# A graph network of four layers: the identity of the third layer added into its adjacency tiles, and a column of logits summed on VectorE

## The chip, the cores and the metric

The kernel runs on one core of one Trainium2 chip, as one program. Its metric is the device time in microseconds, of which the median of several runs is given. A core has TensorE (matrix products, into PSUM), VectorE, ScalarE and GpSimd (element-wise work), and queues that start transfers between the memory of the chip (HBM) and the memory of the core (SBUF). In the profile TensorE is PE, its weight loads are PEld, VectorE is DVE, ScalarE is ACT.

## What is computed

Four layers on 4096 nodes with 128 features each, over one 4096 × 4096 adjacency matrix; each layer's result is added to its input and normalised by rows. The first layer is a hyperbolic attention, the second an attention with four heads. The change is in the third, a convolution, and in what prepares the fourth, an attention with additive logits. From the reference:

```python
def _L2_gnn_ref(x, adj, weight):                  # the third layer
    n = adj.shape[0]
    adj_hat = adj + jnp.eye(n, dtype=adj.dtype)
    deg = jnp.sum(adj_hat, axis=1)
    d_inv_sqrt = (deg + 1e-08) ** (-0.5)
    support = d_inv_sqrt[:, None] * adj_hat * d_inv_sqrt[None, :]
    out = jnp.matmul(jnp.matmul(support, x), weight)
    return jax.nn.relu(out)

def _L3_gnn_ref(X, A, W, b, a_s, a_r):            # the fourth layer
    H = X @ W.T + b
    s = H @ a_s
    r = H @ a_r
    e = jax.nn.leaky_relu(A * s + A * r.T, negative_slope=ALPHA)
    masked = jnp.where(A > 0, e, NEG)
    att = jax.nn.softmax(masked, axis=1)
    return att @ H

# each layer: x = _layernorm(x + layer(x), axis=-1)
```

Two things matter. The third layer uses the adjacency plus the identity. And the fourth layer needs, for every node, the two scalars `s` and `r`; `r` is X times the vector `W.T @ a_r`, plus a constant.

## The kernel before

The adjacency lies in HBM as 8 × 8 tiles of 512 × 512, `adjT[I, J]`, each 1 MB: 128 partitions by four blocks of 512. A ring of eight tiles in SBUF is filled ahead. For each row of tiles I, `convolve` sums over J into one PSUM tile `pa` of 128 features by 512 nodes. `Y` holds the features, scaled by the inverse square root of the degree. The identity of `adj_hat` is added by four matmuls of `Y` with a 128 × 128 identity at the start of the row. `odd` looks, for half of the tiles, whether all entries are 0 or 1.

```python
def convolve(I, J):
    if J == 0:
        st["pa"] = open_sums()
        for b in range(4):
            nc.tensor.matmul(                                              # L1326
                st["pa"][:, b * P : (b + 1) * P], lhsT=Y[:, 4 * I + b, :], rhs=self.ident,
                start=(b == 0), stop=False, skip_group_check=True,
            )
    at = ring[:, (NS * I + J) % RING, :, :]
    for jb in range(4):
        nc.tensor.matmul(                                                  # L1332
            st["pa"], lhsT=Y[:, 4 * J + jb, :], rhs=at[:, jb, :],
            start=False, stop=(J == NS - 1 and jb == 3), skip_group_check=True,
        )
    if J < NS // 2:
        odd = rot.tile([P, 4, S], F32, tag="odd", name="odd", bufs=1)
        n = 2 * NT + NS // 2 * I + J
        nc.vector.scalar_tensor_tensor(                                    # L1340
            odd, at, 0.0, at, op0=ALU.not_equal, op1=ALU.not_equal, accum_out=self.odd[:, n : n + 1]
        )
```

A finished row is worked up in pieces, one piece after each of the tiles J = 0, 1, 2, 3, 5, 6 of the next row:

```python
def finish(I):
    ...
    nc.scalar.copy(a, st["pa"])                                            # L1369, after J = 7
    yield
    pb = ps_b.tile([P, 4, D], F32, tag="pb", name="pb")
    for b in range(4):                                                     # L1373, after J = 0
        nc.tensor.matmul(pb[:, b, :], lhsT=a[:, b * P : (b + 1) * P], rhs=w, start=True, stop=True)
    ...                                                                    # o = relu(d * pb), on ScalarE
    yield
    nc.vector.tensor_tensor(x, x, o, ALU.add)                              # L1378, after J = 1
    for b in range(4):
        self.row_stats(4 * I + b)
    nc.vector.tensor_scalar(rs, self.mv[:, tl, 1], EPS_LN, None, op0=ALU.add)   # L1381
    ...                                                                    # rs = rs ** -0.5, on ScalarE
    yield
    for b in range(4):                                                     # L1387, after J = 2
        ...                                                                # X = (X - mean) * rs
    yield
    for b in range(4):                                                     # L1393, after J = 3
        nc.tensor.transpose(p[:, b, :], X[:, 4 * I + b, :], self.ident)
    nc.scalar.activation(XT, p..., AF.Identity, accum_out=part[:, I : I + 1])
    nc.vector.tensor_tensor(XB[:, tl, :], x, br..., ALU.add)               # L1395
    yield
    pr = ps_s.tile([P, S], F32, tag="ps", name="pr")                       # after J = 5
    for b in range(4):
        nc.tensor.matmul(                                                  # L1399
            pr[:, b : b + 1], lhsT=XT[:, b * P : (b + 1) * P], rhs=ur, start=True, stop=True
        )
    ps = ps_s.tile([P, S], F32, tag="ps", name="psr")
    nc.tensor.matmul(ps, lhsT=us, rhs=XT, start=True, stop=True)           # L1403
    nc.vector.tensor_scalar(r, pr[:, 0:4], cb[:, 1:2], 2.0 * LIMIT, op0=ALU.add, op1=ALU.min)   # L1405
    ...
    nc.vector.tensor_scalar(rho[:, s], ps, cb[:, 0:1], 2.0 * LIMIT, op0=ALU.add, op1=ALU.min)   # L1408
    nc.vector.tensor_reduce(mx[...], rho[:, s], AX.X, ALU.max, apply_absolute_value=True)       # L1409
    ...
    yield
    ...                                                                    # F = X * exp(r), after J = 6
```

The loop runs over 64 tiles of the third layer and then the first eight tiles of the fourth (`attend_first`, L1352 and L1355), during which the last row of the third is finished:

```python
for g in range(groups):                       # groups = NS * NS + NS = 72
    I, J = g // NS, g % NS
    if I < NS:
        convolve(I, J)
    else:
        attend_first(J)
    load(g + RING - 1)
    if g == 2:
        weights()                             # us, ur, cb; L1292 to L1304
    ...
    if J in (0, 1, 2, 3, 5, 6):
        next(rest, None)
    if J == NS - 1 and I < NS:
        rest = finish(I)
        next(rest)
```

Of the kernel before, what the change touches and what calls it, by code (L numbers as in the profile page):

```python
# [9 lines left out]
F32 = mybir.dt.float32  # L10
F32R = mybir.dt.float32r
AF = mybir.ActivationFunctionType
ALU = mybir.AluOpType
# [3 lines left out]
P = 128  # L17
# [7 lines left out]
S = 512  # L25
SAFE = 60.0
LIMIT = 20.0
# [14 lines left out]
class Net:  # L42
# [1201 lines left out]
    def layers23(self, w2, weight, bias, a_s, a_r, out, Y):  # L1244
# [5 lines left out]
        nc, tc, N, NT, NS, D, X = self.nc, self.tc, self.N, self.NT, self.NS, self.D, self.X  # L1250
        with ExitStack() as ctx:
            RING = 8
# [12 lines left out]
            pre = pctx.enter_context(tc.tile_pool(name="pre3", bufs=1))  # L1265
# [11 lines left out]
                nc.sync.dma_start(out=ac[:, k : k + 1], in_=v.unsqueeze(1))  # L1277
            us = pre.tile([P, P], F32, tag="us", name="us")
            ur = pre.tile([P, 1], F32, tag="ur", name="ur")
            cb = pre.tile([P, 2], F32, tag="cb", name="cb")  # L1280
            wt = pre.tile([P, P], F32, tag="wtr", name="wtr")
            last = pre.tile([P, P], F32, tag="last", name="last")
# [4 lines left out]
            st = {}  # L1287

            def weights():

                p = ps_t.tile([P, 4, P], F32, tag="pt", name="pu")
                nc.tensor.matmul(p[:, 0, 0:2], lhsT=wn, rhs=ac[:, 0:2], start=True, stop=True)  # L1292
                nc.tensor.matmul(
                    p[:, 1, 0:2], lhsT=ac[:, 2:3].to_broadcast([P, P]), rhs=ac[:, 0:2], start=True, stop=True
                )
                nc.vector.tensor_copy(us, p[:, 0, 0:1].to_broadcast([P, P]))
                nc.vector.tensor_copy(ur, p[:, 0, 1:2])
                nc.vector.tensor_copy(cb, p[:, 1, 0:2])


                p = ps_t.tile([P, 4, P], F32, tag="pt", name="pw")
                nc.tensor.transpose(p[:, 0, :], wn, self.ident)
                nc.vector.tensor_copy(wt, p[:, 0, :])
                nc.vector.tensor_copy(last, self.ident[:, D - 1 : D].to_broadcast([P, P]))  # L1304
                st["pw"] = p
# [12 lines left out]
            def open_sums():  # L1318
                return ps_a.tile([P, S], F32, tag="pa", name="pa")

            def convolve(I, J):

                if J == 0:
                    st["pa"] = open_sums()
                    for b in range(4):
                        nc.tensor.matmul(  # L1326
                            st["pa"][:, b * P : (b + 1) * P], lhsT=Y[:, 4 * I + b, :], rhs=self.ident,
                            start=(b == 0), stop=False, skip_group_check=True,
                        )
                at = ring[:, (NS * I + J) % RING, :, :]  # L1330
                for jb in range(4):
                    nc.tensor.matmul(  # L1332
                        st["pa"], lhsT=Y[:, 4 * J + jb, :], rhs=at[:, jb, :],
                        start=False, stop=(J == NS - 1 and jb == 3), skip_group_check=True,
                    )
                if J < NS // 2:

                    odd = rot.tile([P, 4, S], F32, tag="odd", name="odd", bufs=1)
                    n = 2 * NT + NS // 2 * I + J
                    nc.vector.scalar_tensor_tensor(  # L1340
                        odd, at, 0.0, at, op0=ALU.not_equal, op1=ALU.not_equal, accum_out=self.odd[:, n : n + 1]
                    )

            def attend_first(J):

# [13 lines left out]
            def finish(I):  # L1359


                s, tl = slice(I * S, (I + 1) * S), slice(4 * I, 4 * I + 4)
                x = X[:, tl, :]
                a = rot.tile([P, S], F32, tag="a", name="a")
                o = rot.tile([P, 4, D], F32, tag="o", name="o")
                rs = rot.tile([P, 4], F32, tag="rs", name="rs")
                XT = rot.tile([P, S], F32, tag="XT", name="XT")
                r = rot.tile([P, 4], F32, tag="r", name="r")
                nc.scalar.copy(a, st["pa"])  # L1369
# [5 lines that stand above are left out]
                    t = 4 * I + b  # L1375
                    nc.scalar.activation(o[:, b, :], pb[:, b, :], AF.Relu, scale=d[:, t : t + 1])
                yield
                nc.vector.tensor_tensor(x, x, o, ALU.add)  # L1378
# [3 lines that stand above are left out]
                nc.scalar.activation(rs, rs, AF.Ln)  # L1382
                nc.scalar.activation(rs, rs, AF.Exp, scale=-0.5)
                yield
                for b in range(4):
                    t = 4 * I + b
                    nc.vector.tensor_scalar(  # L1387
                        X[:, t, :], X[:, t, :], self.mv[:, t, 0:1], rs[:, b : b + 1], op0=ALU.subtract, op1=ALU.mult
                    )
                yield  # L1390
                p = ps_t.tile([P, 4, P], F32, tag="pt", name="pt")
                for b in range(4):
                    nc.tensor.transpose(p[:, b, :], X[:, 4 * I + b, :], self.ident)  # L1393
                nc.scalar.activation(XT, p.rearrange("p a b -> p (a b)"), AF.Identity, accum_out=part[:, I : I + 1])
                nc.vector.tensor_tensor(XB[:, tl, :], x, br.unsqueeze(1).to_broadcast([P, 4, D]), ALU.add)  # L1395
                yield
                pr = ps_s.tile([P, S], F32, tag="ps", name="pr")
                for b in range(4):
                    nc.tensor.matmul(  # L1399
                        pr[:, b : b + 1], lhsT=XT[:, b * P : (b + 1) * P], rhs=ur, start=True, stop=True  # L1400
                    )
                ps = ps_s.tile([P, S], F32, tag="ps", name="psr")
                nc.tensor.matmul(ps, lhsT=us, rhs=XT, start=True, stop=True)  # L1403

                nc.vector.tensor_scalar(r, pr[:, 0:4], cb[:, 1:2], 2.0 * LIMIT, op0=ALU.add, op1=ALU.min)  # L1405
                nc.vector.tensor_scalar(r, r, -2.0 * LIMIT, None, op0=ALU.max)
                nc.vector.tensor_reduce(mx[:, I : I + 1], r, AX.X, ALU.max, apply_absolute_value=True)
                nc.vector.tensor_scalar(rho[:, s], ps, cb[:, 0:1], 2.0 * LIMIT, op0=ALU.add, op1=ALU.min)  # L1408
                nc.vector.tensor_reduce(  # L1409
                    mx[:, NS + I : NS + I + 1], rho[:, s], AX.X, ALU.max, apply_absolute_value=True  # L1410
                )
                nc.scalar.activation(col[:, 0, tl], r, AF.Exp, scale=-0.8)
                nc.scalar.activation(col[:, 1, tl], r, AF.Exp)
                nc.scalar.activation(rho[:, s], rho[:, s], AF.Exp, scale=0.8)
                yield
                for t in range(4 * I, 4 * I + 4):
                    nc.scalar.activation(F[:, t, 0 : D - 1], X[:, t, 0 : D - 1], AF.Copy, scale=col[:, 1, t : t + 1])
                nc.vector.tensor_copy(F[:, tl, D - 1], col[:, 1, tl])
# [19 lines left out]
            with tc.manual_schedule():  # L1438
                nc.scalar.preload_act_table_set("natural_log_exp_and_others")
                for g in range(RING - 1):  # L1440
                    load(g)
                for g in range(groups):
                    I, J = g // NS, g % NS
                    if I < NS:
                        convolve(I, J)
                    else:
# [3 lines that stand above are left out]
                        weights()  # L1450
                    if g == 4:
                        weights_last()
# [6 lines that stand above are left out]
                    if g == groups - 2:  # L1459
                        close_first()  # L1460
                nc.tensor.matmul(st["pa3"], lhsT=tot, rhs=eps, start=False, stop=True, skip_group_check=True)
                nc.scalar.copy(a0, st["pa3"])
# [166 lines left out]
```

## Time and profile before

| | |
|---|---|
| time, median of 3 runs | 2186.93 us (2184.12 to 2188.29) |
| span in the profile | 2182.5 us |
| TensorE busy | 2000.2 us, 92% |
| VectorE busy | 1849.3 us, 85% |
| ScalarE busy | 1458.3 us, 67% |
| third layer, from its first matmul to the first of the fourth layer | 1675.5 to 1926.8 us |
| tile matmuls (L1332) | 512 records, mean 594 ns, no idle time before them |
| identity matmuls (L1326) | 64 records, median 275 ns |
| column of logits (L1399) | 64 records, median 250 ns |

A record is one instruction as the profiler saw it; a matmul in fp32 of this kernel shows as two records, and records of neighbouring matmuls overlap, so the cost of a matmul is read from one start to the next and not from its duration. In the chain of work that ended last, each piece is what the piece after it had to wait for; a piece counts for the time only if it stands there.

### The profile page before, as it was taken

The page shows a single profiled execution, that of the slowest core. Times are in us where ns is not written, and L with a number is a line of the kernel's source. Part 1 is how long each engine was busy: PE and PEld are TensorE (multiplying, and loading weights), DVE is VectorE, ACT ScalarE, POOL GpSimd, SP SyncE. Part 2 cuts the span into 40 slices and gives each one's busy share as a digit, 9 for nine tenths or more (in the row PEclk, how much of TensorE's full clock was granted, in tenths as well). Part 3 has the DMA queues.
Part 4 walks back from the last instruction along what each step waited for, and adds up shares of the span by engine and source line. Part 5 has one row for each costly group of instructions (what it writes and reads, how often), then busy time and mean ns, then how long its engine had stood idle before and what let it go on. Part 6 is the DMA issues. An engine that isn't in the chain of part 4 may idle for free.

```text
span 2182.5 us, 24442 instructions
## 1 busy us (share of the span) xinstructions
PE 2000.2 (92%) x8876; PEld 1066.8 (49%) x8876; DVE 1849.3 (85%) x2700; ACT 1458.3 (67%) x1847; POOL 120.4 (6%) x204
## 2 busy tenths in 40 slices
PE   4699999999999717999999999999997999999998
PEld 4267767776766605333333333333333444544443
DVE  6699999999999887789899999999898454568887
ACT  5699999999999783787878787887883222210000
POOL 2100000000000022210000000000000000000000
PEclk8599999999999957999999999999999999999999
DMA  3166666666666407984645565564555877767783
GB/s 94 55 238 225 214 218 227 217 227 210 210 243 208 159 1 251 240 223 174 193 170 179 175 202 178 176 192 174 175 193 208 312 265 273 261 247 285 288 296 112
DMA packets 114455, 446.77 MB, mean 205 GB/s; under 512 B 12108, under 2 KB 22508, under 8 KB 73360
## 3 DMA queue, kind: packets, MB, share of 16 engines
q1 hardware_dynamic: 93120, 359.77, 46.6%
q10 hardware_dynamic: 9360, 68.16, 9.2%
q0 software_dynamic: 11840, 17.13, 4.4%
q8 instruction: 74, 1.21, 0.2%
q14 instruction: 61, 0.50, 0.1%
HBM read 367.34 MB, written 77.68 MB: 204 GB/s over the span
## 4 chain that ended last, share of the span: by engine, by line
PE 43%; DVE 31%; ACT 16%; DMA 5%; issue 4%; SPq 0%; POOL 0%; ACTq 0%; DVEq 0%; POOLq 0%
PE pa L1332 10%; PE pv L994 10%; PE pa L1512 9%; DVE e L977 8%; PE ps L968 6%; ACT e L975 4%; DVE w L686 3%; DMA adjT<-at 2%; ACT w L674 2%; DVE nat L958 2%; DVE w L718 2%; DVE t L705 2%; DVE w L729 2%; DVE t L666 2%; DVE at L645 2%
## 5 line engine op out<-in xcount | busy, mean ns | idle before, releaser
L977 DVE SCALAR_TENSOR_TENSOR e<-at,e 128x2048 f32<-128x2048 f32 x256 | 582.9, 2287 | 69.6 <-ACT e L975 68.9
L975 ACT ACTIVATE e<-ps 128x1024 f32<-128x1024 f32 x512 | 493.2, 1024 | 145.6 <-PE ps L968 126.0
L994 PE MATMUL pv<-e,VA 128*64 128x512 f32 x2048 | 495.8, 605 | 6.4 <-DVE e L977 6.0
L968 PE MATMUL ps<-QS,KS 128*128 128x512 f32 x1024 | 313.5, 425 | 5.2 <-ACT e L975 3.0
L968 PEld LDWEIGHTS ps<-QS,KS 128*128 128x128 f32 x1024 | 171.3, 189 | 230.2 <-ACT e L975 174.8
L994 PEld LDWEIGHTS pv<-e,VA 128*64 128x64 f32 x2048 | 124.6, 136 | 249.3 <-issue 214.9
L1332 PE MATMUL pa<-ring,Y 128*128 128x512 f32 x512 | 225.8, 594 | 0.0
L1512 PE MATMUL pa<-w,F 128*128 128x512 f32 x448 | 195.3, 594 | 0.0
L1509 DVE SCALAR_TENSOR_TENSOR w<-rho,col,ring 128x512 f32<-128x512 f32 x224 | 162.7, 745 | 22.9 <-PE pa L1512 10.3
L641 PE MATMUL ptA<-ident,ad 128*128 128x128 f32 x1024 | 154.0, 280 | 16.2 <-DMA ad<-in_adj_dram 9.4
L657 PE MATMUL pz<-HT 128*128 128x512 f32 x288 | 159.8, 638 | 1.5 <-DVE e L463 0.9
L741 PE MATMUL pi<-HA,w 128*128 128x129 f32 x1152 | 154.5, 282 | 2.8 <-DVE w L718 2.8
L1332 PEld LDWEIGHTS pa<-ring,Y 128*128 128x128 f32 x512 | 96.0, 191 | 111.5 <-issue 111.3
L741 PEld LDWEIGHTS pi<-HA,w 128*128 128x128 f32 x1152 | 138.2, 193 | 20.5 <-issue 17.2
L686 DVE TENSOR_TENSOR w<-w,at 128x2048 f32<-128x2048 f32 x64 | 146.3, 2285 | 0.0
L1512 PEld LDWEIGHTS pa<-w,F 128*128 128x128 f32 x448 | 83.7, 190 | 106.1 <-issue 77.6
L641 PEld LDWEIGHTS ptA<-ident,ad 128*128 128x128 f32 x1024 | 119.0, 143 | 29.5 <-issue 15.7
L949 ACT ACTIVATE nat<-nat 128x2048 f32<-128x2048 f32 x64 | 122.6, 1916 | 3.9 <-DMA nat<-in_adj_dram 3.8
L666 DVE TENSOR_SCALAR t<-pz 128x512 f32<-128x512 f32 x144 | 96.1, 686 | 16.5 <-PE pz L660 12.8
L756 PE MATMUL pj<-HA,w 128*128 128x129 f32 x896 | 109.7, 275 | 0.1
L756 PEld LDWEIGHTS pj<-HA,w 128*128 128x128 f32 x896 | 104.4, 191 | 0.7 <-DVE X L770 0.3
L645 DVE COPY at<-ptA 128x512 f32<-128x512 f32 x128 | 87.2, 686 | 11.9 <-PE ptA L641 7.1
(392 smaller groups left out, 2514.7 us busy)
## 6 DMA issues: line engine op xcount, KB each, us to landing
ring<-adjT SPq DMA_DIRECT2D x128, 1024.0 KB, 4.9
ad<-in_adj_dram SPq DMA_DIRECT2D x64, 1024.0 KB, 7.1
adjT<-at SPq DMA_DIRECT2D x64, 1024.0 KB, 6.1
nat<-in_adj_dram ACTq DMA_DIRECT2D x64, 1024.0 KB, 4.9
at<-adjT SPq DMA_DIRECT2D x63, 1024.0 KB, 4.8
qk<-cut SPq DMA_DIRECT2D x16, 512.0 KB, 11.7
KS<-qk POOLq DMA_DIRECT2D x32, 256.0 KB, 7.4
QS<-qk POOLq DMA_DIRECT2D x32, 256.0 KB, 5.7
```

Source lines behind the costliest of these rows:

```text
L641: nc.tensor.transpose(pt[:, ib, :], ad[:, ib, jb * P : (jb + 1) * P], self.ident)
L657: nc.tensor.matmul(pz, lhsT=HT[:, j * P : (j + 1) * P], rhs=HT[:, I * S : (I + 1) * S], start=True, stop=False)
L686: nc.vector.tensor_tensor(w, w, st[p][f"at{k}"], ALU.mult)
L741: nc.tensor.matmul(row[I, "po"][ib // 2][:, ib % 2, :], lhsT=st[p]["w0"][:, jb, ib * P : (ib + 1) * P], rhs=HA[:, 4 * J + jb, :], start=False,
L756: nc.tensor.matmul(pj[:, a, :], lhsT=st[p]["w1"][:, ib, jb * P : (jb + 1) * P], rhs=HA[:, 4 * I + ib, :], start=(ib == 0), stop=(ib == 3),)
L968: nc.tensor.matmul(p[:, h, :], lhsT=KS[:, h2 + h, jb * P : (jb + 1) * P], rhs=QS[I % 2][:, h2 + h, :], start=True, stop=True,)
L975: nc.scalar.activation(e[:, h2 : h2 + 2, :], p, AF.Exp)
L977: nc.vector.scalar_tensor_tensor(e, at[:, jb % 4, :].unsqueeze(1).to_broadcast([P, NH, S]), 0.0, e, op0=ALU.not_equal, op1=ALU.mult,)
L994: nc.tensor.matmul(st["po"][h // 2][g : g + 64, :], lhsT=VA[:, o : o + 64], rhs=e[:, h, :], start=(jb == 0), stop=(jb == NT - 1), skip_gro ...
L1332: nc.tensor.matmul(st["pa"], lhsT=Y[:, 4 * J + jb, :], rhs=at[:, jb, :], start=False, stop=(J == NS - 1 and jb == 3), skip_group_check=True,)
L1509: nc.vector.scalar_tensor_tensor(w, rho[:, I * S : (I + 1) * S], col[:, 0, j : j + 1], at[:, jb, :], op0=ALU.max, op1=ALU.mult)
L1512: nc.tensor.matmul(pa, lhsT=F[:, j, :], rhs=w, start=False, stop=(j == NT - 1), skip_group_check=True)
```

## The change

The identity leaves TensorE for all rows but the first: VectorE adds it to the four 128 × 128 blocks on the diagonal of the diagonal tile, in the ring, before the matmuls of that tile read it. The order for it is given one tile ahead. The look for entries other than 0 and 1 has to come before the addition, so it is moved for the diagonal tiles of rows 1 to 3 (later diagonal tiles aren't looked at). The column `r` of the fourth layer's logits is summed by VectorE, as the sum over features of X times a row `urr`, for all rows but the last; `urr` is made once by one more matmul. Both are meant to take small matmuls off TensorE.

```diff
+                nc.tensor.matmul(p[:, 2, :], lhsT=ac[:, 1:2].to_broadcast([P, P]), rhs=wn, start=True, stop=True)
+                nc.vector.tensor_copy(urr, p[:, 2, :])
 ...
+            def look(I, J):
+                at = ring[:, (NS * I + J) % RING, :, :]
+                odd = rot.tile([P, 4, S], F32, tag="odd", name="odd", bufs=1)
+                n = 2 * NT + NS // 2 * I + J
+                nc.vector.scalar_tensor_tensor(
+                    odd, at, 0.0, at, op0=ALU.not_equal, op1=ALU.not_equal, accum_out=self.odd[:, n : n + 1]
+                )
+
+            def diagonal(I):
+                at = ring[:, (NS * I + I) % RING, :, :]
+                if I < NS // 2:
+                    look(I, I)
+                for b in range(4):
+                    a = at[:, b, b * P : (b + 1) * P]
+                    nc.vector.tensor_tensor(a, a, self.ident, ALU.add)
+
             def convolve(I, J):
                 if J == 0:
                     st["pa"] = open_sums()
+                if I == J == 0:
                     for b in range(4):
                         nc.tensor.matmul(
-                            st["pa"][:, b * P : (b + 1) * P], lhsT=Y[:, 4 * I + b, :], rhs=self.ident,
+                            st["pa"][:, b * P : (b + 1) * P], lhsT=Y[:, b, :], rhs=self.ident,
                             start=(b == 0), stop=False, skip_group_check=True,
                         )
                 at = ring[:, (NS * I + J) % RING, :, :]
                 for jb in range(4):
+                    j = 4 * J + jb
                     nc.tensor.matmul(
-                        st["pa"], lhsT=Y[:, 4 * J + jb, :], rhs=at[:, jb, :],
-                        start=False, stop=(J == NS - 1 and jb == 3), skip_group_check=True,
-                    )
-                if J < NS // 2:
-                    (the look, as above)
+                        st["pa"], lhsT=Y[:, j, :], rhs=at[:, jb, :], start=(I > 0 and j == 0), stop=(j == NT - 1),
+                        skip_group_check=True,
+                    )
+                if J < NS // 2 and (J != I or I == 0):
+                    look(I, J)
 ...  (in finish)
-                pr = ps_s.tile([P, S], F32, tag="ps", name="pr")
-                for b in range(4):
-                    nc.tensor.matmul(
-                        pr[:, b : b + 1], lhsT=XT[:, b * P : (b + 1) * P], rhs=ur, start=True, stop=True
-                    )
+                if I < NS - 1:
+                    ra = rot.tile([P, 4], F32, tag="ra", name="ra")
+                    for b in range(4):
+                        nc.vector.scalar_tensor_tensor(
+                            o[:, b, :], X[:, 4 * I + b, :], 1.0, urr, op0=ALU.mult, op1=ALU.mult,
+                            accum_out=ra[:, b : b + 1],
+                        )
+                else:
+                    ra = ps_s.tile([P, S], F32, tag="ps", name="pr")
+                    (the four matmuls, as before)
 ...  (in the loop, ahead of convolve)
+                    if 0 < (g + 1) // NS == (g + 1) % NS < NS:
+                        diagonal((g + 1) // NS)
```

More of the change, by code (lines that the diff above doesn't have):

```diff
@@ L1279, in layers23 @@
             ur = pre.tile([P, 1], F32, tag="ur", name="ur")
+            urr = pre.tile([P, P], F32, tag="urr", name="urr")
             cb = pre.tile([P, 2], F32, tag="cb", name="cb")
@@ L1331, in convolve @@
                 for jb in range(4):
+                    j = 4 * J + jb
                     nc.tensor.matmul(
-                        st["pa"], lhsT=Y[:, 4 * J + jb, :], rhs=at[:, jb, :],
-                        start=False, stop=(J == NS - 1 and jb == 3), skip_group_check=True,
-                    )
-                if J < NS // 2:
[L1338 to L1341, printed above, removed]
-                    )
+                        st["pa"], lhsT=Y[:, j, :], rhs=at[:, jb, :], start=(I > 0 and j == 0), stop=(j == NT - 1),
+                        skip_group_check=True,
+                    )
+                if J < NS // 2 and (J != I or I == 0):
+                    look(I, J)
             def attend_first(J):
@@ L1396, in finish @@
                 yield
-                pr = ps_s.tile([P, S], F32, tag="ps", name="pr")
-                for b in range(4):
-                    nc.tensor.matmul(
-                        pr[:, b : b + 1], lhsT=XT[:, b * P : (b + 1) * P], rhs=ur, start=True, stop=True
-                    )
+                if I < NS - 1:
[7 more added lines that the diff above has]
+                    ra = ps_s.tile([P, S], F32, tag="ps", name="pr")
+                    for b in range(4):
+                        nc.tensor.matmul(
+                            ra[:, b : b + 1], lhsT=XT[:, b * P : (b + 1) * P], rhs=ur, start=True, stop=True
+                        )
                 ps = ps_s.tile([P, S], F32, tag="ps", name="psr")
                 nc.tensor.matmul(ps, lhsT=us, rhs=XT, start=True, stop=True)
-                nc.vector.tensor_scalar(r, pr[:, 0:4], cb[:, 1:2], 2.0 * LIMIT, op0=ALU.add, op1=ALU.min)
+                nc.vector.tensor_scalar(r, ra[:, 0:4], cb[:, 1:2], 2.0 * LIMIT, op0=ALU.add, op1=ALU.min)
                 nc.vector.tensor_scalar(r, r, -2.0 * LIMIT, None, op0=ALU.max)
```

## The prediction

> **What bounds the kernel now.** I read the profile from coarse to fine: first the slices of the span, to find the stage that the change touches; then the chain of work that ended last, inside that stage; then the waits of TensorE there; last the order of time on VectorE, because that is where the removed work goes.
>
> The change touches lines 1326, 1332, 1340 and 1399, and the profile places all of them between 1675 and 1961 us: the third layer, in eight rows of eight tiles. The table by stretches gives (columns: stretch, its length, then busy us of PE, weight loads, VectorE, ScalarE, GpSimd, the granted clock, DMA share, GB/s):
>
> ```profile
> 1675.00:1707.00 32.00, 31.51 (x84) 15.65 (x85) 17.24 (x31) 0.88 (x5) 0.00 (x0) 0.93 0.98 396
> 1707.00:1927.00 220.00, 220.00 (x657) 108.99 (x656) 103.32 (x203) 53.73 (x128) 0.00 (x0) 1.00 0.75 268
> 1927.00:1961.00 34.00, 29.60 (x80) 13.29 (x78) 24.17 (x52) 7.57 (x19) 0.00 (x0) 0.95 0.69 253
> ```
>
> In the middle stretch, rows 1 to 7, TensorE is busy for all of its 220 us at full clock; VectorE is busy for 103, under half. The transfers run at 268 GB/s, while the first stretch, in which the ring is filled, shows 396: the memory has room.
>
> A busy TensorE is not yet a bounding one, since its records are long and overlap. So the second view: the chain that ended last, for the stretch of one whole row (columns: start, us, what):
>
> ```profile
> 1706.68 0.89 PE pa L1326 x8
> 1707.57 3.44 PE pa L1332 x8
> 1711.00 0.89 PE pb L1373 x8
> 1711.89 10.30 PE pa L1332 x24
> 1722.20 0.44 PE pt L1393 x4
> 1722.63 6.87 PE pa L1332 x16
> 1729.50 0.79 PE pr L1399 x8
> 1730.29 0.97 PE psr L1403 x2
> 1731.26 6.87 PE pa L1332 x16
> 1738.12 0.11 PE pa L1326
> ```
>
> Nothing but TensorE is on it, piece after piece without a gap. One row, from 1706.68 to 1738.12, takes 31.44 us. The eight tiles are 3.44 + 10.30 + 6.87 + 6.87 = 27.48 us, or 3.43 us for a tile of four matmuls (each appears as two records). The rest is small work between them: the identity matmuls of L1326 (0.89), pb (0.89), the transposes (0.44), pr (0.79) and psr (0.97). The chain repeats these to 0.01 us in all later rows. The third view, who waited for whom in these rows, holds no entry for TensorE's matmuls at all, and one for its weight loads that names another engine:
>
> ```profile
> PEld pt L1393 <- DVE XB L1395: 2.0, 7, 0.3
> ```
>
> That is 0.3 us per row, of the length of an ordinary pause between weight loads there. So this stage is bound by how much TensorE has to issue, and a matmul taken out shortens it one for one, as long as nothing else becomes late.
>
> [...] That is why pr is worth removing: its matmuls have one output column, yet each reloads 128 columns of weights, twice. The trace agrees: eight weight loads of L1399 in a stretch of 0.86 us, 0.107 each. [...] For this change it means that a VectorE instruction queued in front of the identity additions can delay TensorE; the trace of before shows VectorE standing still 8.54 us at L1405 with the next row's work behind it. [...] the trace has 287 ns for the one such addition (L1310).
>
> **The change part by part.**
>
> Removed from TensorE: the four identity matmuls of rows 1 to 7, at 0.89 us a row: 7 × 0.89 = 6.23 us. Removed too: the four pr matmuls in the finishing of rows 0 to 6, which run during rows 1 to 7: 7 × 0.79 = 5.53 us. The finishing of row 7 keeps them (that runs beside the fourth layer's first tiles, where VectorE is the busier engine), and row 0 keeps its identity. Together 11.76 us.
>
> Added to TensorE: one 128-column matmul for the row urr, once. A like one (L1309, two records) took 0.21 us from start to the next matmul. Net on TensorE: 11.76 − 0.21 = 11.55 us, and a row goes from 31.44 to 29.76 us.
>
> Added to VectorE, per row: four additions, some 0.23 us apart and 0.29 for the last, about 1.0 us; four multiply-and-sum instructions in the form of L1035 (291 ns and 82 ns for the read of the sum, 0.33 us from one to the next in the chain), 1.35 us. Some 2.4 us a row on an engine busy for 15.0 of 31 us. It lands at about 17.4 of 29.8: 58%. Once, a copy of urr, 0.29 us. None of this is on the chain unless it comes late.
>
> Moved: in rows 1 to 3 the look at the diagonal tile (2.29 us) now comes before its addition, one tile earlier.
>
> *Does the addition come late?* It is queued at the start of the tile before the diagonal one. I went through the seven rows with the order of the instructions on VectorE. Rows 1 and 2: the additions stand before `X + o`, for which VectorE had waited 11.32 us, so they are done long before. Rows 4 to 6: behind the normalisation or the XB addition, which end 1718.97 and 1721.8 in the row shown, with a tile or more to spare. Row 7: behind the maximum over rho. There psr starts at 1730.15 and VectorE is free at 1732.7; the additions end near 1733.7, and the matmul that needs them would start 0.94 + 3.43 us after psr, at 1734.5. Spare: 0.8 us. Row 3 is the tight one, because look and additions stand behind the row statistics:
>
> ```profile
> 1715.57 0.17 DVE L1381 TENSOR_SCALAR rs<-mv 128x4 f32<-128x4 f32 x1
> 1715.64 2.28 DVE L1340 SCALAR_TENSOR_TENSOR odd<-ring 128x2048 f32<-128x2048 f32 x1
> 1717.85 0.08 DVE L1340 DVE_READ_ACCUMULATOR odd<-ring 128x1 f32 x1
> 1717.85 1.12 DVE L1387 TENSOR_SCALAR X<-X,mv,rs 128x128 f32<-128x128 f32 x4
> ```
>
> In this row's times: look until 1717.9, additions ready at about 1718.2, 1718.4, 1718.65 and 1718.9. The third tile of the stretch that begins at 1711.73 has its first matmul 2 × 3.43 us later, at 1718.6, the next every 0.86 us. Each waits for its own addition, so all four are just in time. But then a second look (until 1721.2) comes before the four normalisations (until about 1722.3), and the transposes want those at 1722.0. I allow 0.3 us, once.
>
> Sum: 11.55 − 0.3 = 11.25 us, rounded to 11.3 with nothing taken for the releases themselves. 2186.93 − 11.3 = 2175.6 us. What follows the stage (the fourth layer) starts earlier by this and is else unchanged.
>
> **The rivals.**
>
> *VectorE delays TensorE in every row.* If each of seven diagonal tiles waited a full look (2.3 us), 16 us would be lost and the kernel would be some 5 us slower: 2191. [...] Against it: the walk above, which finds one tight row.
>
> *The transfers become the bound.* A row's 8 MB must arrive in 29.8 instead of 31.4 us: 268 becomes 283 GB/s. For it: the DMA engines are 75% busy. Against it: 396 GB/s while the ring filled, 4.9 us from issue to landing, seven tiles (24 us) ahead. If the rate were stuck at 268, all would be eaten: 2187.
>
> *Only half is won.* One of the two removals might hide: [...] The chain charges it 0.79 us and the weight loads fill the stretch, so I count it. If it were free, 2181.
>
> **Range and chances.** Three times of before lie between 2184.12 and 2188.29, so a median is good to some 2 us; that, and up to 2 us for waits that I missed, make 2172.5 to 2179.5. The whole removal is 0.5% of the time, so 2% in either direction needs something that no view shows: 2% is 44 us, nearly four times what is removed.
>
> **What would show it.** Right: rows 29.8 us apart in the chain, still TensorE alone; no pieces of the identity or pr between the tiles except in row 0 and in the finishing of row 7; VectorE some 17.4 us busy a row; 283 GB/s. Wrong: waits of the tile matmuls for the additions above 1 us in all, tiles more than 3.44 us long, or a half-clock stretch inside the rows. A shortened chain with an unchanged total would point at the fourth layer, whose start is bound by VectorE in places (L1352 and L1408 stand in its chain).

## Result and profile after

| | before | after |
|---|---|---|
| time, median | 2187.61 us (2184.12 to 2190.61, 4 runs) | 2176.82 us (2173.47 to 2178.11, 4 runs) |
| ratio, 95% interval | | 0.9949 (0.9930 to 0.9968) |
| span of the profiled run | 2182.5 us | 2175.8 us |
| start of the third layer | 1675.49 us | 1681.16 us |
| third layer, to the first matmul of the fourth | 251.30 us | 238.95 us |
| fourth layer, to the end of the span | 255.71 us | 255.69 us |

The kernel is 10.8 us faster, half a per cent. The three lower rows show more than the total does: the third layer alone is 12.35 us shorter, the fourth is unchanged, and in these two profiles the first two layers, whose instructions are the same, differ by 5.67 us to the other side.

The table by stretches of the changed kernel, for seven rows (columns as before: busy us of PE, weight loads, VectorE, ScalarE, GpSimd, clock, DMA share, GB/s):

```profile
1707.00:1915.00 208.00, 208.00 (x548) 96.95 (x547) 112.99 (x278) 51.81 (x123) 0.00 (x0) 1.00 0.80 287
```

TensorE is still busy throughout, at full clock. The transfers have gone from 268 to 287 GB/s. VectorE is busy 54% of this stretch, where it had 47%.

The chain that ended last, for one row:

```profile
1734.44 0.86 PE psr L1430 x2
1735.30 10.30 PE pa L1356 x24
1745.60 0.89 PE pb L1392 x8
1746.49 10.30 PE pa L1356 x24
1756.79 0.44 PE pt L1412 x4
1757.23 6.87 PE pa L1356 x16
1764.09 0.86 PE psr L1430 x2
```

Row to row, from psr to psr, is 29.65 us instead of 31.44. The identity pieces and the pr pieces are gone, all other pieces are as long as before, with one exception: psr, the matmul for the scalars `s` of the fourth layer, takes 0.86 instead of 0.97. Who waited for whom, for the weight loads of this layer:

```profile
PEld pa L1356 <- DVE ring L1341: 0.6, 2, 0.4
PEld pt L1412 <- DVE ring L1341: 0.6, 2, 0.3
```

These are the only entries that name the additions, two weight loads each. None of them reaches a matmul: the same view holds no wait of a tile matmul in these rows, and all row distances agree to 0.01 us.

### The profile page after: what moved, and what is told of

It reads as the page before. It is cut to its first block, busy times and chain, and to the rows that moved or that the text cites. A ratio compares the mean times of both kernels' runs of the same rounds, so it can differ in the third digit from the quotient of the medians.

```text
span 2175.8 us, 24318 instructions
## 1 busy us (share of the span) xinstructions
PE 1994.8 (92%) x8766; PEld 1057.9 (49%) x8766; DVE 1861.7 (86%) x2785; ACT 1458.2 (67%) x1847; POOL 120.1 (6%) x204
## 4 chain that ended last, share of the span: by engine, by line
PE 43%; DVE 32%; ACT 17%; issue 5%; DMA 4%; POOL 0%; ACTq 0%; DVEq 0%; SPq 0%; POOLq 0%
PE pa L1356 10%; PE pv L994 10%; PE pa L1541 9%; DVE e L977 8%; PE ps L968 6%; ACT e L975 4%; DVE w L686 3%; ACT w L674 3%; DVE nat L958 2%; DVE w L718 2%; DVE t L705 2%; DVE w L729 2%; DVE t L666 2%; DVE at L645 2%; ACT nat L949 1%
## 5 line engine op out<-in xcount | busy, mean ns | idle before, releaser
L1538 DVE SCALAR_TENSOR_TENSOR w<-rho,col,ring 128x512 f32<-128x512 f32 x224 | 162.7, 746 | 23.0 <-PE pa L1541 10.3
L674 ACT ACTIVATE w<-di,dr 128x512 f32<-128x512 f32 x144 | 92.1, 712 | 7.4 <-DMA di<-rows 7.3
```

What stands on the lines that cost most here:

```text
L1538: nc.vector.scalar_tensor_tensor(w, rho[:, I * S : (I + 1) * S], col[:, 0, j : j + 1], at[:, jb, :], op0=ALU.max, op1=ALU.mult)
```

## Experiments

None of these kernels leaves work out. Row distances are taken in the chain from psr to psr, third and fourth layer from first matmul to first matmul, in one profile each. The row distances repeat to 0.01 us. The third layer repeats less well, from 238.60 to 239.52 us in four profiles in which it has the same work to do, because it starts at half clock (for 3.79 us in the kernel before, 3.55 in the changed one) and this reaches more or less far into row 0; the table under "Sum" takes that part out. The totals scatter by several us. "Before" had medians of 2187.74 us (36 runs) beside the first four, 2187.24 (29) beside the next four and 2187.64 (11) beside the last three.

### The changed kernel again

No edit.

> The changed kernel once more, for the gap between two numbers: the profiles give 12.35 us for the third layer alone (251.30 us before, 238.95 after, from its first matmul to the first of the fourth layer), the medians 10.8, the profiled spans only 6.7. Theory (the first two layers, whose instructions are the same, vary by some us from run to run): third layer again 238.9 to 239.1 us, its start elsewhere than at 1681.2 us by a few us, fourth layer 255.7 us, and a difference of the medians nearer to 12. Rival (the change costs the first two layers something, by where its code or buffers lie): start again at 1681 and the difference stays near 7 to 10.

Measured: 2176.83 us (7 runs, 2171.27 to 2181.22), ratio 0.9949 (0.9931 to 0.9968). Rows 29.66 us, third layer 239.52, fourth 255.74, start of the third layer at 1683.9. The rows repeat exactly. The third layer is 0.6 us longer, more than the 238.9 to 239.1 that was expected, and all of it in row 0, the only row that runs partly at half clock. The start moved by 2.8 us, but the difference of the medians, 10.9, did not come nearer to 12. The last two runs below come back to this.

### The identity alone

```diff
-                if I < NS - 1:
+                if I < 0:
                     ra = rot.tile([P, 4], F32, tag="ra", name="ra")
...
-                nc.tensor.matmul(p[:, 2, :], lhsT=ac[:, 1:2].to_broadcast([P, P]), rhs=wn, start=True, stop=True)
-                nc.vector.tensor_copy(urr, p[:, 2, :])
```

> Only the identity moves to VectorE; the column of logits stays on TensorE in all rows, and urr isn't made. Theory (each group of four small matmuls in TensorE's stream costs its pieces, whatever they compute): the row goes from 31.44 to 30.55 us, the third layer from 251.3 to 245.1 us, the time by 6.2 us to about 2181. Rival (only one of the two removals counts, the other hides under neighbours): either no gain, or the whole 12.

Measured: rows 30.55 us, third layer 245.40, time 2180.15 us (18 runs), ratio 0.9963 (0.9951 to 0.9975). The removal of the identity is worth its pieces, 0.89 us a row; it neither hides nor brings more. pr and psr stand at 0.79 and 0.97 here, as before.

### The column of logits alone

```diff
-                if I == J == 0:
+                if J == 0:
                     for b in range(4):
                         nc.tensor.matmul(
-                            st["pa"][:, b * P : (b + 1) * P], lhsT=Y[:, b, :], rhs=self.ident,
+                            st["pa"][:, b * P : (b + 1) * P], lhsT=Y[:, 4 * I + b, :], rhs=self.ident,
...
-                    if 0 < (g + 1) // NS == (g + 1) % NS < NS:
-                        diagonal((g + 1) // NS)
```

with the looks back in their old places and no tile matmul opening a sum.

> Only the column of logits moves to VectorE (not for the last row); the identity stays on TensorE in all rows. Theory: the row goes from 31.44 to 30.54 us, by 0.79 for pr and 0.11 that psr is shorter without pr ahead of it (0.86 instead of 0.97); the third layer to 251.3 - 7 x 0.90 + 0.2 = 245.2 us, the time by 6.1 us. Rival (the prediction as it stood: 0.79 a row and psr unchanged): row 30.65, third layer 246.0. Rival (pr is hidden because its matmuls have one column): no gain.

Measured: rows 30.55 us, time 2181.36 us (18 runs), ratio 0.9977 (0.9968 to 0.9986). The rows decide: 31.44 − 30.55 = 0.89 is the theory, not the 0.79 of the prediction. The third layer as a whole was 246.49, which looks like the rival's 246.0, but 1.2 us of that is row 0: the half-clock stretch in which the layer starts lasted 13.7 us here and 10.2 in the kernel before, and reached further into it.

### psr ahead of pr

In the kernel before, the two are swapped:

```diff
-                pr = ps_s.tile([P, S], F32, tag="ps", name="pr")
-                for b in range(4):
-                    nc.tensor.matmul(pr[:, b : b + 1], lhsT=XT[:, b * P : (b + 1) * P], rhs=ur, ...)
                 ps = ps_s.tile([P, S], F32, tag="ps", name="psr")
                 nc.tensor.matmul(ps, lhsT=us, rhs=XT, start=True, stop=True)
+                pr = ps_s.tile([P, S], F32, tag="ps", name="pr")
+                for b in range(4):
+                    nc.tensor.matmul(pr[:, b : b + 1], lhsT=XT[:, b * P : (b + 1) * P], rhs=ur, ...)
```

> The kernel before with psr ahead of the four pr matmuls instead of behind. Theory ([...] it belongs to the group): psr 0.86 us, pr 0.79, the tiles behind 6.87 + 0.11 = 6.98, row unchanged at 31.44 us. Rival (psr was shorter in the changed kernel because something else there made it so): psr stays 0.97 and the tiles 6.87.

Measured (2188.37 us, one run), in the chain of this kernel:

```profile
1733.14 0.86 PE psr L1398 x2
1734.00 0.79 PE pr L1401 x8
1734.79 6.97 PE pa L1332 x16
```

The 0.11 us moved from psr to the tiles behind pr (6.97 instead of 6.87), and the row stayed 31.44 to 31.45. So it belongs to the group of small matmuls: the long matmul behind them, psr or the tile, carries it. What makes it up is not shown. Four small matmuls cost 0.79 + 0.11 = 0.90 us, with one output column each, where the four with 128 columns cost 0.89. The weight loads of the two groups, in the kernel before, look alike:

```profile
1706.52 0.86 PEld L1326 LDWEIGHTS pa<-ident,Y 128*128 128x128 f32 x7 [0.24 <-issue]
1729.34 0.86 PEld L1399 LDWEIGHTS pr<-ur,XT 128*128 128x128 f32 x7 [0.24 <-issue]
```

Seven loads of 0.19 us take 0.86 us in both, so they start 0.11 us apart, and eight such steps make an estimate of 0.9 us for either group, with one output column or with 128.

### No lead for the additions

```diff
-                    if 0 < (g + 1) // NS == (g + 1) % NS < NS:
-                        diagonal((g + 1) // NS)
+                    if 0 < g // NS == g % NS < NS:
+                        diagonal(g // NS)
```

> The changed kernel with the additions given right ahead of the diagonal tile instead of one tile earlier. Theory ([...] what stands ahead of the additions decides): TensorE waits in row 2 about 3.1 us, in row 3 about 3.0, in row 6 about 2.1, and under 0.5 elsewhere: third layer 8 us longer than 239, two thirds of the gain lost. Rival (VectorE has half its time free, so the place in its order doesn't matter): 239 us, no wait above 0.5.

Measured: 2186.39 us (12 runs), ratio 1.0005 (0.9991 to 1.0019). In the time all of the gain is gone; the third layer is 250.56 us, 11.6 more than with the lead and 0.7 less than before. Rows 2 and 3 are 34.60 and 34.29 us, row 6 is 31.69, the others 29.66. TensorE in order of time, at the diagonal tiles of rows 2 and 3 (in brackets the idle time before, and who ended it):

```profile
1749.35 8.83 PE L1356 MATMUL pa<-ring,Y 128*128 128x512 f32 x16 [2.98 <-DVE ring L1341]
...
1787.19 5.28 PE L1356 MATMUL pa<-ring,Y 128*128 128x512 f32 x8 [2.79 <-DVE ring L1341]
```

and in row 6:

```profile
1891.36 4.13 PE L1356 MATMUL pa<-ring,Y 128*128 128x512 f32 x9 [1.76 <-DVE ring L1341]
```

The waits are where the walk through VectorE's order put them, and about as long: 2.98, 2.79 and 1.76 us where 3.1, 3.0 and 2.1 were expected. But sixteen records take 7.03 us elsewhere in this view and 8.83 here, eight take 5.28 instead of 3.60. The table by stretches, around row 2, has a mean clock of 0.91 where the rows otherwise have 1.00:

```profile
1741.00:1760.00 19.00, 16.02 (x43) 7.50 (x42) 10.76 (x34) 4.99 (x12) 0.00 (x0) 0.91 0.58 213
```

The recorded clock is at half for 3.4 us from 1749.4 and again from 1787.0, that is from about the moment at which TensorE resumes. So the row with the wait of 2.98 us is 4.94 us longer, the one with 2.79 is 4.63 longer, and the one with 1.76, at a clock of 1.00 throughout, 2.03. Some 3.5 of the 11.6 us, 8.83 − 7.03 and 5.28 − 3.60, are thus the clock's, and that is the part that the expectation lacked.

### A second look in row 3

```diff
                 if I < NS // 2:
                     look(I, I)
+                if I == 3:
+                    look(I, I)
```

> The changed kernel with the look at the diagonal tile of row 3 done twice (2.2 us more on VectorE, once). Theory (row 3 is just in time, with some 0.3 us to spare): TensorE waits about 1.9 us at the diagonal tile of row 3 and up to 0.3 us at the transposes after it; row 3 is 31.6 to 31.9 us, all other rows 29.66. Rival (there is slack that the walk missed): all rows 29.66.

Measured: row 3 takes 31.85 us, all others 29.66. The chain of this kernel runs through VectorE there:

```profile
1783.15 2.21 DVE odd L1329 x2
1785.37 0.02 issue
1785.39 2.31 DVE odd L1329 x2
1787.70 0.02 issue
1787.72 0.30 DVE ring L1343
1788.03 0.04 issue
1788.07 3.70 PE pa L1358 x8
```

Of 2.24 us more on VectorE 2.19 arrive in the row. So with one look row 3 is really just in time: there the entry of 0.4 us in the view of waits above, where an ordinary pause between weight loads is 0.24, is already a weight load held up by the addition, while its matmul still starts on time. TensorE was idle 1.89 us, and its clock stayed full: the eight records behind the wait took 3.70 us, where eight at half clock took 5.28 in the run without the lead. In the total (2176.42 us, 6 runs, ratio 0.9949, 0.9928 to 0.9969) these 2 us are not seen.

### A ring of four

```diff
-            RING = 8
+            RING = 4
```

> The changed kernel with a ring of four tiles instead of eight, so each tile is loaded three tiles (10.3 us) ahead instead of seven (24 us). Theory (the transfers have room: some 5 us from issue to landing, 387 GB/s while the ring fills): rows within 0.2 us of 29.66, except where VectorE can no longer look ahead: a look that stands behind the row statistics then holds its tile's place in the ring; at most 2 us in all. Rival (at 287 GB/s the transfers are close to the bound, and the deep ring hides it): waits of TensorE or VectorE for the ring's transfers in every row, third layer 5 us longer or more.

Measured: all rows 29.66 us, third layer 238.66, fourth 255.79, 2177.86 us (11 runs), ratio 0.9961 (0.9948 to 0.9974). The 4.8 us from issue to landing fit into three tiles (10.3 us). VectorE now waits for the ring, TensorE doesn't:

```profile
DVE odd L1329 <- DMA ring<-adjT: 14.0, 7, 7.4
```

At 284 GB/s the transfers did not bound this layer; half of the ring would do.

### The last row too

```diff
-                if I < NS - 1:
+                if I < NS:
                     ra = rot.tile([P, 4], F32, tag="ra", name="ra")
```

> The changed kernel with the column of logits summed on VectorE in the last row as well, beside the first tiles of the fourth layer. Theory (VectorE stands idle 3.5 us there, waiting for pr): the stretch from the first matmul of the fourth layer to the end shortens by 0.8 to 0.9 us, from 255.7 to 254.8. Rival (VectorE is the engine that bounds there, so work added to it costs): the stretch grows by up to 1.4 us.

Measured: from the psr of row 6 to that of row 7, which lies among the first tiles of the fourth layer, 31.28 us instead of 32.07; fourth layer 254.88 instead of 255.69; 2174.13 us (7 runs), ratio 0.9947 (0.9927 to 0.9966). VectorE does the sums in time in which it had stood waiting: 3.47 us for pr in the kernel before, still 2.03 us for psr here. The gain of 0.8 us is seen in the pieces, not in the total.

### Every row

Row 0 takes its tiles in the order 1 to 7, 0, and has no identity matmuls; the last row as above.

```diff
+            def tile_of(g):
+                return (g + 1) % NS if g < NS else g % NS
...
-                nc.sync.dma_start(out=ring[:, g % RING, :, :], in_=self.adjT[g // NS % NS, g % NS])
+                nc.sync.dma_start(out=ring[:, g % RING, :, :], in_=self.adjT[g // NS % NS, tile_of(g)])
...
-                if I == J == 0:
-                    (the four identity matmuls of row 0)
...
-                    if 0 < (g + 1) // NS == (g + 1) % NS < NS:
+                    if g + 1 < NS * NS and (g + 1) // NS == tile_of(g + 1):
                         diagonal((g + 1) // NS)
```

> Identity and column of logits on VectorE in every row: as the run with the last row too, and row 0 takes its tiles in the order 1 to 7, 0, so that VectorE has time to look at the tile 0,0 and to add the identity before TensorE needs it. Theory (row 0's four identity matmuls are on the path too): the third layer starts with a tile instead, and is shorter by the 2.07 us that they took at half clock, less what the half clock then takes from the first tiles instead: 1 to 2 us less than 238.6; the time 2 to 3 us under the changed kernel's in all. Rival (the identity matmuls of row 0 fill a time in which TensorE would wait for the first tile or for Y anyway): third layer 238.6 as before, gain 0.8 us from the last row alone.

Measured: 2173.24 us (6 runs, 2166.78 to 2177.06), ratio 0.9933 (0.9917 to 0.9950). The layer starts with tiles:

```profile
1681.67 12.27 PE pa L1353 x24
```

where the changed kernel has 2.08 us of identity and then 11.10. Third layer 238.04 us, 0.91 less than the changed kernel and 0.56 less than the run before: less than the 1 to 2 expected. Between those two the reach of the half clock differs; with it taken out as in the table under "Sum" the layer is 236.31 us instead of 237.17, so 0.86 less. The identity took 2.08 us at a recorded clock of 0.50 in the changed kernel, and in this run the stretch at half clock falls on the tiles; what is won is about the price at full clock, 0.89. Against the changed kernel that is 0.9 us in row 0 and 0.8 in the last. It is the fastest version of the study by its median; its interval overlaps that of the changed kernel, so only the pieces show that it is faster.

### The kernel before, twice more

No edit.

> The kernel before, for the time at which the third layer starts: in the profiles so far 1675.5 and 1678.8 us in two kernels without the change, 1672.9 to 1686.2 in eight with some of it. Theory (the first two layers vary by themselves): somewhere in 1672 to 1687. Rival (the change delays them by some 4 us): again under 1679.

> As the run before this one, a second sample: theory 1672 to 1687, rival under 1679.

Measured (2191.27 and 2185.86 us, one run each): start of the third layer at 1682.6 and 1677.9 us; rows 31.44 to 31.45 in both. The rival asked for both under 1679, and one is not. The four kernels without any of the change now start at 1675.5 to 1682.6 (mean 1678.7), the nine with some of it at 1672.9 to 1686.2 (mean 1681.6). The start goes largely with the time that TensorE's clock was at half in the first 1660 us: 157.0 us for a start at 1672.9, 160.4 for 1675.5, 177.5 for 1681.2, 184.3 for 1686.2. Less half of that time, as an estimate of what the half clock lost, the mean start is 1593.8 without any of the change and 1593.6 with some of it, over 1590.8 to 1595.8 in all thirteen. So apart from the clock no delay is seen. The time at half clock itself was 160.4 to 177.5 us in the four kernels without the change and 157.0 to 184.3 in the nine with it. Nothing in the instructions explains the 6 us between the two means (169.8 and 176.0), and whether it is more than chance stays open.

## Why the prediction was right

**What bounds.** Right. The chain holds TensorE alone in the rows before and after, and each half of the change, done alone, moved the row by its own pieces: 31.44 to 30.55 either way, 29.65 with both. The row was expected at 29.76; the missing 0.11 belong to the pr matmuls, below.

**The identity, 7 × 0.89.** Right: 0.89 a row in the run that does it alone.

**The pr matmuls, 7 × 0.79.** Mis-sized. The term is 7 × 0.90, because the psr matmul behind them had 0.11 us of theirs in its own piece. I had read the cost of a group from its own line in the chain; the swap of psr and pr shows that 0.11 follows the group to whatever comes next. The rival "only half is won", by which a pr matmul might be free, falls with the same runs. The reading of the weight loads was slightly off: it is seven of L1399, not eight, that fill the 0.86 us, and they start 0.11 us apart, not 0.107.

**urr and the additions on VectorE.** The urr matmul is in the chain with 0.33 us instead of 0.21; read with its neighbours, the group of small matmuls around it takes 0.77 us instead of 0.51, so it costs 0.26. In one row (1734.44 to 1764.09) VectorE is busy 16.87 us, I had 17.4: the four additions take 0.90 us and the four sums 0.94, not 1.0 and 1.35, since the sums start 0.21 us apart and not 0.33. L1310, given as an addition of the same form, is a subtraction that reads PSUM; the additions themselves last 280 to 293 ns, median 284, where L1310 has 287.

**Row 3, 0.3 us.** Not paid. The prediction placed the additions at the last moment and the transposes 0.3 us late; the first was right, as the second look shows, and the second didn't happen: row 3 is as long as the others. In the changed kernel:

```profile
1785.24 1.11 DVE L1406 TENSOR_SCALAR X<-X,mv,rs 128x128 f32<-128x128 f32 x4
1786.28 0.60 PE L1412 MATMUL pt<-ident,X 128*128 128x128 f32 x4
```

The last normalisation ends at 1786.35, after the first transpose has started. But each transpose reads one block of 128 columns only, and each block was ready in time. The prediction had let the first transpose wait for all four.

**Sum.** For the third layer I had 11.25 us. Its two corrected terms give 7 × (0.89 + 0.90) = 12.53, less 0.26 = 12.27; the profiles have 12.35. The layer starts at half clock, for 3.79 us before and 3.55 after, counted from its first matmul; with half of that taken off, profiles of the same work agree to 0.02 us:

| kernels | third layer, us | less half of its time at half clock |
|---|---|---|
| before, its two later samples, psr ahead of pr | 251.30, 251.15, 252.08, 251.67 | 249.40 to 249.41 |
| identity alone | 245.40 | 243.15 |
| column of logits alone | 246.49 | 243.42 |
| changed, again, ring of four, last row too | 238.95, 239.52, 238.66, 238.60 | 237.16 to 237.18 |

So the layer gains 12.23 us, the identity alone 6.26 and the column alone 5.99: the two add up. The time moved by 10.8, inside an interval that reaches from 7 to 15. That the estimate for the time, 11.3, came so near is in part luck: the layer gained 1.0 us more than I said, and the medians show 1.4 us less than the layer. This last difference lies within the interval of the medians; its cause is not shown.

**The rivals.** "VectorE delays TensorE in every row" fails as the order stands, and the run without the lead shows how near it lies: one tile later in VectorE's order, and three rows wait, at a cost of 11.6 us. The prediction had put the loss of that rival at 2.3 us a row without a thought of the clock. "The transfers become the bound": no, 287 GB/s are delivered, and with half the ring still 284.

## What to carry over

Where the chain showed TensorE alone, the pieces taken from it were won in full (a row went from 31.44 to 29.65 us); but read a group of small matmuls together with the piece behind it, for a matmul with one output column costs here what one with 128 does (0.90 and 0.89 us for four). Work that moved to an engine with time to spare was free only at the right place in its order: here one tile of lead is worth 11.6 of the 12.35 us. And measure such a change by the distance between repeated pieces, which agree to 0.01 us, when the totals scatter by ten or more.

## What was not expected

A wait of TensorE for VectorE of 2.98 or 2.79 us was followed by 3.4 us at half clock, which cost another 1.7 to 1.8 us; waits of 1.89 and 1.76 us were not. The changes of the recorded clock lie on a grid: in the kernel before all 21, in the changed one all 19 are whole numbers of steps of 3.4133 us apart, to 0.02 us, and the two half-clock stretches of the run without the lead begin 11 steps apart. A window is here one such step. The window ahead of the half clock was not idle throughout: it held 0.43 us of matmuls at the wait of 2.98 and 0.83 at that of 2.79; the one around the wait of 1.76 held 1.65, and the wait of 1.89 fell into two windows, which held 2.35 and 2.59.

So in these profiles the place of a wait on the grid counts as well as its length. The fourth layer shows it. TensorE waits there for VectorE for 2.22 us in the kernel before and for 2.23 us in its second later sample. Two windows in each, the busy time of TensorE first after the length, the clock third from the end:

```profile
1952.35:1955.76 3.41, 1.44 (x4) 0.72 (x5) 3.38 (x6) 1.80 (x5) 0.00 (x0) 1.00 0.00 0
1955.76:1959.17 3.41, 3.41 (x6) 1.33 (x5) 1.12 (x6) 0.00 (x0) 0.00 (x0) 0.50 0.44 168
...
1952.91:1956.32 3.41, 2.38 (x12) 1.27 (x10) 1.51 (x5) 0.30 (x2) 0.00 (x0) 1.00 0.61 257
1956.32:1959.73 3.41, 2.22 (x5) 1.05 (x6) 3.41 (x8) 1.80 (x5) 0.00 (x0) 1.00 0.00 0
```

In the first the wait leaves one window 58% idle, and half clock follows; in the second it is shared out, 30% and 35%, and the clock stays full. In the third and fourth layers of all thirteen profiles the windows at full clock that half clock followed were idle, by the matmul records, for 54% or more, and the others for 56% at most; the two ranges overlap, and no exact limit is shown. Without the last row's column on VectorE, the fourth layer took 255.7 to 256.2 us where it holds such a half-clock stretch and 254.0 to 254.1 where it holds none. The kernel before got either with the same instructions: 255.71 us in its first profile, 254.0 in its second later sample.
